# Attention over 4096 positions: energies in three float32r passes, with q and k streamed from HBM

## The chip, the cores and the metric

The kernel runs on one core of a Trainium2 chip. The metric is the device time of one execution in microseconds (us). Runs were called fast at a mean granted clock of 0.98 or more (the granted clock is the share of its full clock that TensorE gets). Names used below: TensorE (PE) multiplies matrices into PSUM, a memory of banks, VectorE (DVE) and ScalarE (ACT) work element by element, GpSimd (POOL) issues some of the DMAs. PEld is TensorE's loading of weights. A ring is a set of buffers used in turn. float32r is a form of float32 whose matmuls cost TensorE less. A "record" is one line of the trace for one executed instruction.

## The reference

```python
B, W, H, C = x.shape            # 4, 64, 64, 256
N = W * H                       # 4096
q = einsum('bwhc,cd->bwhd', x, Wq) + bq      # d = 128
k = einsum('bwhc,cd->bwhd', x, Wk) + bk
v = einsum('bwhc,cd->bwhd', x, Wv) + bv
pq, pk, pv = (t.reshape(B, -1, N) for t in (q, k, v))
energy = einsum('bcn,bcm->bnm', pq, pk)
attention = softmax(energy, axis=-1)
out = einsum('bcm,bnm->bcn', pv, attention).reshape(B, W, H, C)
return gamma * out + x
```

## The kernel before

Each of the 4 images is projected first (16 iterations of transpose, qk, v). Then 16 groups of 256 columns follow, each of 8 steps of 512 keys, so 512 steps in all. A step makes energies in full f32 (4 matmuls), exponentiates them on ScalarE, splits the result into float32r parts `h`, `l`, `d`, and multiplies these with the parts of v (24 matmuls). At a group's end the two sums are scaled, transposed and added to x. The program itself sets the order of work on every engine.

```python
ps_s = pool("ps_s", 4, space=PSUM)     # four one-bank score buffers
ps_o = pool("ps_o", 1, space=PSUM)     # four accumulators a0 b0 a1 b1
# ... (cut)
def energy(b, u):
    # ...
    for k in range(2):
        sp = ps_s.tile([P, 2, NB], F32, tag="s", ...)
        for i in range(2):
            nc.tensor.matmul(sp[:, i, :], pr.pk[:, 4 * t + 2 * k + i, :],
                             pr.pqf[:, g * NB : (g + 1) * NB], start=True, stop=True)
        nc.scalar.activation(x[:, 2 * k : 2 * k + 2, :], sp, AF.Exp)
    nc.scalar.activation(h, x, AF.Identity, scale=UPPER)
# ... (cut)
for u in range(STEPS):
    if u + LOOK < STEPS:
        energy(b, u + LOOK)
    proceed()                  # one piece of the finish of an earlier group
    if u + 1 < STEPS:
        halves(b, u + 1)       # l and d of the next step, VectorE
    attend(b, u)               # 24 matmuls; scales the sums at a group's end
    proceed()
```

## Time and profile before

| | before |
|---|---|
| time, median | 2666.6 us |
| TensorE busy | 2639 us, 99% |
| VectorE / ScalarE busy | 1507 us / 1334 us (57% / 50%) |
| one step of 8 energy records and 24 attention matmuls | 4.58 us |
| one group of 8 steps | 37.22 us |
| one iteration of the projection | 3.89 us |
| from an image's first to its last scaling of sums | 556.6 us |
| from there to the next image's first | 104.1 us |

The prediction shows how the page is read. The slices of the span add one thing, that nothing varies over the run except the DMA's work in the four projections (each digit is a fortieth of the span in tenths; PEclk is the granted clock of TensorE):

```profile
PE   8999999999999999999999999999999999999998
PEclk9999999999999999999999999999999999999999
DMA  2000000000200000000020000000002000000000
```

### The profile page before, as it was taken

Reading aid. Unit: us, or ns where it says so; the run is one execution under the profiler, and the core shown is the slowest. Engines: PE = TensorE matmul, PEld = TensorE weight load, DVE = VectorE, ACT = ScalarE, POOL = GpSimd, SP = SyncE. Lnnn points to the kernel's source line nnn. Section 1 sums busy time; section 2 is a strip of 40 time slices with the busy share of each in tenths; the row PEclk is TensorE's granted clock in tenths of the full one; section 3 lists DMA queues with packets and bytes.
Section 4 is the critical chain, followed back from the end, with each engine's and each line's share of the span. In section 5 each row is a group of like instructions: output and inputs, shape, how many; then the busy total and the mean of one; then the engine's idle time right before and its main releaser. Section 6 shows DMA issues by size and latency. Waiting matters only on the chain.

```text
span 2665.1 us, 42006 instructions
## 1 busy us (share of the span) xinstructions
PE 2639.4 (99%) x17922; PEld 2486.4 (93%) x17922; DVE 1506.8 (57%) x1993; ACT 1333.7 (50%) x1922; POOL 44.8 (2%) x70
## 2 busy tenths in 40 slices
PE   8999999999999999999999999999999999999998
PEld 7999999999899999999989999999998999999998
DVE  3555555555465555555545555555555555555555
ACT  3555555455455455455445555455545555545543
POOL 0000000000000000000000000000000000000000
PEclk9999999999999999999999999999999999999999
DMA  2000000000200000000020000000002000000000
GB/s 89 9 16 10 17 17 17 13 13 17 72 9 17 13 13 16 17 17 9 17 72 9 17 17 9 17 17 17 17 17 64 9 17 17 17 9 17 17 9 10
DMA packets 41667, 53.76 MB, mean 20 GB/s; under 512 B 3584, under 2 KB 37376, under 8 KB 41472
## 3 DMA queue, kind: packets, MB, share of 16 engines
q1 hardware_dynamic: 34816, 33.56, 4.1%
q0 software_dynamic: 5120, 16.78, 1.8%
q8 instruction: 142, 2.33, 0.3%
q10 hardware_dynamic: 1536, 0.66, 0.1%
q14 instruction: 53, 0.43, 0.0%
HBM read 34.21 MB, written 16.78 MB: 19 GB/s over the span
## 4 chain that ended last, share of the span: by engine, by line
PE 98%; DVE 1%; ACT 0%; DMA 0%; issue 0%; POOL 0%; ACTq 0%
PE a L294 37%; PE s L250 33%; PE b L294 18%; PE qk L136 4%; PE v L156 4%; PE ot L330 1%; PE xt L123 1%; DMA bv_sb<-in_L_conv_bv_dram 0%; DVE d L268 0%; DVE l L265 0%; ACT v L165 0%; ACT o L319 0%; DMA wqk_sb<-in_L_conv_Wk_dram 0%; DVE vl L238 0%; ACT vh L235 0%; DVE o L322 0%
## 5 line engine op out<-in xcount | busy, mean ns | idle before, releaser
L294 PE MATMUL a<-vh,h 128*128 128x258 f32 x4096 | 1242.3, 303 | 0.0
L294 PE MATMUL a<-vl,l 128*128 128x258 f32 x4096 | 1156.2, 282 | 1.9 <-DVE l L265 1.9
L294 PE MATMUL b<-vd,d 128*128 128x256 f32 x4096 | 1151.3, 281 | 3.0 <-DVE d L268 3.0
L257 ACT ACTIVATE x<-s 128x512 f32<-128x512 f32 x1024 | 610.5, 597 | 1056.2 <-PE s L250 1042.6
L265 DVE TENSOR_TENSOR l<-x,h 128x1024 fp32r<-128x1024 f32 x512 | 626.5, 1224 | 844.4 <-issue 841.8
L250 PE MATMUL s<-pq,pk 128*128 128x256 f32 x4096 | 966.5, 379 | 0.0
L250 PEld LDWEIGHTS s<-pq,pk 128*128 128x128 f32 x4096 | 741.2, 190 | 80.3
L294 PEld LDWEIGHTS a<-vl,l 128*128 128x128 f32 x4096 | 773.1, 189 | 14.5 <-DVE l L265 3.1
L294 PEld LDWEIGHTS a<-vh,h 128*128 128x128 f32 x4096 | 773.6, 189 | 11.5
L294 PEld LDWEIGHTS b<-vd,d 128*128 128x128 f32 x4096 | 774.0, 189 | 3.8 <-DVE d L268 3.8
L268 DVE SCALAR_TENSOR_TENSOR d<-h,x 128x1024 fp32r<-128x1024 f32 x512 | 623.9, 1219 | 0.0
L259 ACT ACTIVATE h<-x 128x1024 fp32r<-128x1024 f32 x512 | 542.7, 1060 | 16.3
L136 PE MATMUL qk<-wqk_sb,xts 128*128 128x256 f32 x512 | 123.5, 385 | 7.7 <-ACT xts L129 7.7
L156 PE MATMUL v<-xts,wv_sb 128*128 128x256 f32 x512 | 119.7, 379 | 0.0
L319 ACT ACTIVATE o<-b,r 128x256 f32<-128x256 f32 x128 | 60.6, 474 | 108.2 <-DVE r L313 108.2
L136 PEld LDWEIGHTS qk<-wqk_sb,xts 128*128 128x128 f32 x512 | 93.9, 193 | 19.4 <-ACT xts L129 8.8
L156 PEld LDWEIGHTS v<-xts,wv_sb 128*128 128x128 f32 x512 | 97.3, 190 | 13.2
L238 DVE SCALAR_TENSOR_TENSOR vl<-vh,v 128x512 fp32r<-128x512 f32 x64 | 44.4, 693 | 113.1 <-ACT vh L235 113.1
L165 ACT ACTIVATE v<-v,bv_sb 128x256 f32<-128x256 f32 x128 | 53.6, 469 | 105.6 <-PE v L156 105.6
L322 DVE SCALAR_TENSOR_TENSOR o<-a,r,o 128x256 f32<-128x256 f32 x128 | 62.0, 484 | 52.6 <-ACT o L319 52.6
L334 POOL DMA_DIRECT2D out_dram<-x x64 | 44.1, 690 | 2613.3 <-DVE x L333 2575.5
L333 DVE TENSOR_TENSOR x<-x,ot 128x512 f32<-128x512 f32 x64 | 44.0, 687 | 39.1 <-PE ot L330 39.1
(32 smaller groups left out, 406.1 us busy)
## 6 DMA issues: line engine op xcount, KB each, us to landing
x<-in_x_dram SPq DMA_DIRECT2D x128, 256.0 KB, 2.9
out_dram<-x POOLq DMA_DIRECT2D x64, 256.0 KB, 2.5
wv_sb<-in_L_conv_Wv_dram ACTq DMA_DIRECT2D x1, 256.0 KB, 4.4
wqk_sb<-in_L_conv_Wq_dram ACTq DMA_DIRECT2D x1, 128.0 KB, 2.1
wqk_sb<-in_L_conv_Wk_dram ACTq DMA_DIRECT2D x1, 128.0 KB, 3.1
bqk_sb<-in_L_conv_bq_dram ACTq DMA_DIRECT2D x1, 64.0 KB, 5.5
bqk_sb<-in_L_conv_bk_dram ACTq DMA_DIRECT2D x1, 64.0 KB, 5.8
bv_sb<-in_L_conv_bv_dram ACTq DMA_DIRECT2D x2, 0.5 KB, 5.1
```

What stands on the lines that cost most here:

```text
L136: nc.tensor.matmul(qk[:, s, :], self.xt[i][:, k, s, :], wqk_sb[:, k, :], start=(k == 0), stop=(k == KC - 1),)
L156: nc.tensor.matmul(vp[:, eh, :], wv_sb[:, k, eh * P : (eh + 1) * P], self.xt[i][:, k].rearrange("p s a -> p (s a)"), start=(k == 0), stop= ...
L165: nc.scalar.activation(to[:, eh, :], vp[:, eh, :], AF.Identity, bias=bias[:, eh : eh + 1], scale=scale,)
L238: nc.vector.scalar_tensor_tensor(t[:, m, :C], h.bitcast(F32), -f, v4, ALU.mult, ALU.add)
L250: nc.tensor.matmul(sp[:, i, :], pr.pk[:, 4 * t + 2 * k + i, :], pr.pqf[:, g * NB : (g + 1) * NB], start=True, stop=True,)
L257: nc.scalar.activation(x[:, 2 * k : 2 * k + 2, :], sp, AF.Exp)
L259: nc.scalar.activation(h, x, AF.Identity, scale=UPPER)
L265: nc.vector.tensor_tensor(l, x, h.bitcast(F32), ALU.subtract)
L268: nc.vector.scalar_tensor_tensor(d, h.bitcast(F32), 1.0 + E, x, ALU.mult, ALU.subtract)
L294: nc.tensor.matmul(out_, left[:, i, n], right[:, m, :], start=(m == 0 and first), stop=(m == NM - 1 and last),)
L319: nc.scalar.activation(o[:, j, :], bb, AF.Identity, scale=r[:, 0, j : j + 1])
L322: nc.vector.scalar_tensor_tensor(o[:, j, :], a[:, :C], r[:, 1, j : j + 1], o[:, j, :], ALU.mult, ALU.add)
```

## The change

The intent is to take the energies out of full f32. q and k are each split into an upper half and two differences ("forms"). Three float32r products then give two sums, `sa` and `sb`, and the exponential of the energy is the product of two exponentials. The three forms of k and of q aren't kept on the chip: the projection writes them to HBM and each step loads its k forms (768 KB). The score ring of four PSUM banks becomes two rings of two. The order at a group's end changes: the halves of the next step now come between the two halves of `attend`. Two settings change too: energies run three steps ahead instead of two (LOOK), and v lags the qk of the projection by one iteration instead of three (LAG), so one v instead of three is left for an image's start.

```diff
-        ps_s = pool("ps_s", 4, space=PSUM)
+        ppool, work, kpool = pool("ppool", 2), pool("work", 2), pool("kpool", 3)
+        dram = pool("dram", 2, space=DRAM)
+        ps_s = pool("ps_s", 2, space=PSUM)
 ... (cut)
+        def project_qk(b, i):
+            ...
+            nc.scalar.activation(h, x, AF.Identity, scale=UPPER / 64)
+            for j, s, op in ((1, -64.0, ALU.add), (2, 64.0 * (1.0 + E), ALU.subtract)):
+                nc.vector.scalar_tensor_tensor(f[:, :, j, :], h.bitcast(F32), s, x, ALU.mult, op)
+            nc.gpsimd.dma_start(kf[b][i // 2, :, i % 2], f[:, 1])
+            nc.gpsimd.dma_start(qf[b]..., f[:, 0])
 ... (cut)
+            for i in range(2):
+                for to, f, first, last in ((sa, 0, True, False), (sa, 1, False, True), (sb, 2, True, True)):
+                    nc.tensor.matmul(to[:, i], kt[:, 2 * k + i, f, :], q[:, :, f, :], start=first, stop=last)
+            for to, sp, scale in ((x, sa, (1.0 + E) / E), (y, sb, -1.0 / E)):
+                nc.scalar.activation(to[...], sp, AF.Exp, scale=scale)
+        def join(b, u):
+            nc.vector.tensor_tensor(x, x, y, ALU.mult)
 ... (cut: start of an image)
+            load_q(b, 0)
+            for u in range(3):
+                load_k(b, u)
 ... (cut: the loop of steps)
+                if ahead < STEPS:
+                    energy(b, ahead, 0)
+                if u + 2 < STEPS:
+                    join(b, u + 2)
+                    upper(b, u + 2)
                 proceed()
+                attend(b, u, 0)            # at a group's end: scales half j=0
                 if u + 1 < STEPS:
                     halves(b, u + 1)
-                attend(b, u)
+                if ahead < STEPS:
+                    energy(b, ahead, 1)
+                    load_k(b, ahead + 2)
                 proceed()
+                attend(b, u, 1)            # at a group's end: scales half j=1
```

## The prediction

> **What bounds the kernel now.** I read the page's busy shares first, then the chain of work that ended last, then the costliest groups, and last the timeline of one steady stretch. From the page:
>
> ```profile
> PE 2639.4 (99%) x17922; PEld 2486.4 (93%) x17922; DVE 1506.8 (57%) x1993; ACT 1333.7 (50%) x1922; POOL 44.8 (2%) x70
> ...
> PE 98%; DVE 1%; ACT 0%; DMA 0%; issue 0%; POOL 0%; ACTq 0%
> ...
> L294 PE MATMUL a<-vh,h 128*128 128x258 f32 x4096 | 1242.3, 303 | 0.0
> ...
> L257 ACT ACTIVATE x<-s 128x512 f32<-128x512 f32 x1024 | 610.5, 597 | 1056.2 <-PE s L250 1042.6
> L265 DVE TENSOR_TENSOR l<-x,h 128x1024 fp32r<-128x1024 f32 x512 | 626.5, 1224 | 844.4 <-issue 841.8
> L250 PE MATMUL s<-pq,pk 128*128 128x256 f32 x4096 | 966.5, 379 | 0.0
> ```
>
> TensorE is the bound and waits for almost nothing (idle 0.0 before its groups); 98% of the ending chain is TensorE. VectorE and ScalarE are idle nearly half the time, waiting for it. A mean of 303 or 379 ns is a pipelined duration, not a cost, so I price matmuls by start-to-start distance. The TensorE timeline of one step (512 steps in all: 4 images x 16 groups x 8):
>
> ```profile
> 1006.59 1.89 PE L250 MATMUL s<-pq,pk 128*128 128x256 f32 x8
> ...
> 1011.17 1.89 PE L250 MATMUL s<-pq,pk 128*128 128x256 f32 x8
> ```
>
> A step takes 4.58 us. Its 8 energy records are 4 program matmuls (2048 in the source, 4096 records); the chain gives such a run 1.73 us, so one f32 matmul costs 0.433 us. The other 2.85 us are 24 float32r matmuls: 0.119 us each. Eight steps and one output transpose (about 0.6 us) make 37.22 us, the distance between the like points 1001.45 and 1038.67; no wait shows in it. An image takes 663.5 us (first qk matmuls at 674.18 and 1337.68): 16 groups are 595.5, the projection 16 x 3.89 = 62.2, start and drain some 5.
>
> VectorE at the end of a group, where the sums are scaled:
>
> ```profile
> 1037.32 0.16 DVE L311 COPY zall<-a 128x1 f32<-128x1 f32 x1 [0.74 <-PE a L294]
> ...
> 1038.48 0.48 DVE L322 SCALAR_TENSOR_TENSOR o<-a,r,o 128x256 f32<-128x256 f32 x1 [0.41 <-ACT o L319]
> 1038.88 0.15 DVE L311 COPY zall<-a 128x1 f32<-128x1 f32 x1
> ...
> 1041.14 0.69 DVE L333 TENSOR_TENSOR x<-x,ot 128x512 f32<-128x512 f32 x1 [0.64 <-PE ot L330]
> 1041.75 1.22 DVE L265 TENSOR_TENSOR l<-x,h 128x1024 fp32r<-128x1024 f32 x1
> 1042.88 1.22 DVE L268 SCALAR_TENSOR_TENSOR d<-h,x 128x1024 fp32r<-128x1024 f32 x1
> ```
>
> One scaling holds VectorE in order for 1.56 us (1037.32 to 1038.88), 0.4 of it waiting for ScalarE. A 1024-wide operation costs 1.135 us back to back (1041.75 to 1042.88). Today TensorE doesn't feel this, because halves for the next step are ready long before.
>
> **What the Trainium skill says.** "FP8 and Floating Point Precision", TensorE Precision Notes: true FP32 takes four passes through the array. Here 0.433 against 0.119 us is a ratio of 3.65; the trace agrees roughly, as each float32r matmul costs some 0.01 us more than its share. "PSUM — Partial Sum Buffer", Specifications: eight banks of 512 FP32 values. The kernel before has four one-bank score buffers and four accumulators, so two kinds of score force the rings down to two each. "VectorE: DVE Perf Modes", The TRN2 errata: an fp32 tensor-tensor takes (N+151)/0.96 ns, 1224 ns at N = 1024; the trace shows 1224 ns, so I use it for the new product. "DMA: Bandwidth & Descriptors", Anatomy of one DMA: some 2.0 us plus bytes/436 GB/s on the GpSimd path, 2.6 us for 256 KB; the trace's stores landed in 2.5 us.
>
> **The change, part by part.**
>
> 1. Energies. 4 f32 matmuls (1.73 us) become 12 float32r ones (12 x 0.119 = 1.42). TensorE's step is 4.27 us, 0.305 less; x 512 = **-156 us**. This is the whole intended gain.
>
> 2. ScalarE per step: 4 exponentials instead of 2. 4 x 0.597 + 1.06 = 3.45 us of 4.27. Hidden, 0.8 to spare. VectorE per step: product, l and d, 3 x 1.135 = 3.41 us. Hidden in mid-group. Over a group VectorE has 27.2 + 2 x 1.56 + 0.61 = 31.0 us of some 34.8: no bound on average, but close.
>
> 3. End of a group. Program order on VectorE is now: product for u+2, scaling of half j=0 (after TensorE ends that half), **then** the halves for u+1, then scaling of j=1. I worked one group with the durations above, time 0 being the start of the last step's energies. TensorE ends half j=0 at 0.71 + 1.42 = 2.14. VectorE, done with the product at 1.3, waits; it scales from 2.29 to 3.85, makes l to 5.07 and d to 6.2. TensorE wants d at 4.27 + 0.71 + 0.24 = 5.2 and gets it at 6.3: 1.1 us lost. Then VectorE scales j=1 from 6.12 to 7.68; ScalarE's o for it stands in the queue in front of the next exponentials, which come at 7.25 instead of about 5. Product of u+3 to 8.9, its h to 10.1, second pair of exponentials to 11.1. Meanwhile the transpose has taken a slot of the two-deep "b" ring, so the next energies need just that second pair: 0.2 to 0.5 us lost there and as much at the transpose. Step u+3 starts at 15.2; 3 x 4.27 + 0.6 = 13.4 would be free of waits. Some 1.8 us per group; for the 60 group ends inside an image **+108 us**.
>
> 4. Projection. Transposes, qk and v share a ring of two banks. The next qk needs the bank that v used: two ScalarE copies, released about 0.2 + 0.84 + 0.05 = 1.09 us after v ends, while the transpose between covers 0.43. 0.66 us x 15 x 4 = **+40 us**. The new h and two differences per iteration (ScalarE 0.6, VectorE 1.2 us more) fit in 4.5 us.
>
> 5. Start of an image. Before, energies followed the last qk at once. Now: bias add 0.9 us, h 0.7, two differences 1.3, four GpSimd issues (0.7 each in the trace), then two writes and two loads, 2.0 MB, at the 350 GB/s that the stores show (16.78 MB in 1.8% of the span) 5.6 us, and landing: about 10.5 us after the last qk, of which v covers 1.7. Then exponentials, product, h and halves of the first units run nearly in series, some 11 us with 6 us of matmuls in them. About 8.7 + 5 us idle, less what start and drain cost today: +12 us, x 4 = **+48 us**. A cold clock after the gap could add a little.
>
> 6. Streaming. One k load is 786 KB a step, q 393 KB a group: 0.4 GB, 190 GB/s of the 350 seen. A buffer comes free and is asked for more than two steps ahead (some 10 us), against an estimated 2 + 1.8 + queueing: hidden.
>
> Sum: 2666.6 - 156 + 108 + 40 + 48 = **2707 us**.
>
> **Rivals.**
> - A: TensorE stays fed, only the projection and the start cost something: 2666.6 - 156 + 60 = about 2570. For it: 99% busy before, and averages of 80 to 90% on the other engines leave room. Against it: at the group's end the room is 1.2 us and the delay over 2.
> - B: VectorE becomes the bound through most of a group, as its 31 us plus waits grow past TensorE's: 2750 to 2800. For it: two waits for TensorE and ScalarE per group stand in its order. Against it: mid-group it regains 0.86 us a step, so it recovers in three steps.
> - C: the loads don't keep up (casting to float32r on the way, or slow issue). If a load took over 4.3 us in the stream, every step would wait, and the time would leave the range upward. The trace shows stores of that path at 350 GB/s, no loads.
>
> **Range and chances.** The -156 us is the firmest term. The 108 may be 60 to 140 (the 1.1 us wait for d follows from order alone), the 40 from 20 to 55, the 48 from 25 to 80. These put most of the weight from 2615 to 2770. I widen downward, since a schedule so deliberately split may have been tuned to avoid what I see. Range 2585 to 2775. Faster by over 2% means under 2613: 0.23. Slower means over 2720: 0.35.
>
> **What will tell.** Energy groups of 12 matmuls 1.42 us long confirm part 1. Part 3 shows as TensorE waiting for d or l about 1 us just after each group's end, with smaller waits for PSUM a step later, and the eight-step period near 36.6 instead of 37.22; a period of 34.8 refutes it. Part 4 shows as an iteration of about 4.5 us instead of 3.89. Part 5 shows as a TensorE gap of 8 to 12 us between an image's last v matmuls and its first energies, with DMA as releaser. TensorE waiting for k loads in mid-group would make the whole sum wrong.

## The result, and the profile after

The changed kernel takes 2742.5 us (median of 4, 2741.7 to 2744.8) against 2666.4 us (median of 4) in the same rounds: ratio 1.0288, 95% interval 1.0270 to 1.0305, slower. (Ratios here are the mean time of one kernel's fast runs over the mean of the other's in the same rounds, so not quite the ratio of the medians.) The result is correct.

The page of the changed kernel, its busy shares, chain, slices, and the groups that answer to those shown of before:

```profile
PE 2539.8 (93%) x19970; PEld 2461.6 (90%) x19970; DVE 2159.8 (79%) x2568; ACT 1809.9 (66%) x3010; POOL 443.0 (16%) x774
...
PE   7799999999979999999987999999998799999998
...
PEclk9899999999999999999998999999999899999999
DMA  6666556665666665566476666665647566666653
...
PE 65%; DVE 13%; ACT 13%; DMA 5%; issue 3%; POOL 1%; ACTq 0%; SPq 0%; DVEq 0%; POOLq 0%
...
L308 DVE TENSOR_TENSOR x<-x,y 128x1024 f32<-128x1024 f32 x512 | 626.2, 1223 | 265.6 <-ACT y L298 265.6
...
k<-kf POOLq DMA_DIRECT2D x512, 768.0 KB, 4.7
```

TensorE is busy 100 us less than before, yet the run is 76 us longer: the chain that ended last is now only 65% TensorE, with 13% each of VectorE and ScalarE, and 5% DMA. No engine is a bound on average. The time is lost in waits, and the slices say where to look first: TensorE's 7s and 8s stand at the four image starts, and its clock is a little lower at three of them.

In the stream, the intended gain is there. A step in mid-group takes 4.26 us (two energies' starts 883.22 and 887.48), where 4.27 was predicted and 4.58 was before. A typical group takes 36.4 us instead of 37.22 (the median distance of like points; below, 824.20 to 860.59), so most of what the steps gain is lost again inside the group. VectorE's timeline around the end of one group, in order of start (start, duration, then what ended the idle time before it):

```profile
824.20 0.16 DVE L365 COPY zall<-a 128x1 f32<-128x1 f32 x1 [1.20 <-PE a L347]
...
858.16 1.23 DVE L308 TENSOR_TENSOR x<-x,y 128x1024 f32<-128x1024 f32 x1 [0.78 <-ACT y L298]
860.59 0.16 DVE L365 COPY zall<-a 128x1 f32<-128x1 f32 x1 [1.20 <-PE a L347]
...
861.74 0.48 DVE L370 SCALAR_TENSOR_TENSOR o<-a,r,o 128x256 f32<-128x256 f32 x1 [0.41 <-ACT o L369]
862.14 1.21 DVE L319 TENSOR_TENSOR l<-x,h 128x1024 fp32r<-128x1024 f32 x1
863.28 1.22 DVE L322 SCALAR_TENSOR_TENSOR d<-h,x 128x1024 fp32r<-128x1024 f32 x1
864.41 0.15 DVE L365 COPY zall<-a 128x1 f32<-128x1 f32 x1
```

And TensorE's timeline at the same place:

```profile
864.64 0.36 PE L347 MATMUL b<-vd,d 128*128 128x256 f32 x1 [0.84 <-DVE zall L365]
...
869.35 0.39 PE L294 MATMUL sb<-q,k 128*128 128x256 f32 x1 [0.48 <-ACT y L298]
```

VectorE sits idle for 1.20 us until TensorE has ended half j=0, then scales it, and only then makes `l` and `d`. `d` ends at 864.50 (863.28 + 1.22), and TensorE's first matmul with it starts 0.14 us later. The reader names the small copy `zall`, which came last by its count, but the matmul reads `d`. A step later the energies wait for a bank of the `sb` ring until ScalarE has exponentiated it. In start times these two cost TensorE about 1.1 and 0.6 us per group (the idle time in the bracket is less, since the end of a matmul is modelled).

The other part lies between the streams. From the reciprocals' start times, summed over the run:

| part | before, us | after, us | difference |
|---|---|---|---|
| start of the run to image 0's first scaling | 116.1 | 144.2 | +28.1 |
| first to last scaling, four images | 2226.4 | 2189.4 | -37.0 |
| last scaling to the next image's first, three times | 312.4 | 395.2 | +82.8 |
| last scaling to the end | 10.1 | 12.7 | +2.6 |
| span of the profiled runs | 2665.1 | 2741.5 | +76.4 |

In these parts the projection's iteration is 4.65 us instead of 3.89, with this wait each time (TensorE's timeline, two lines of before and two of after):

```profile
43.82 1.89 PE L136 MATMUL qk<-wqk_sb,xts 128*128 128x256 f32 x8
...
47.71 1.89 PE L136 MATMUL qk<-wqk_sb,xts 128*128 128x256 f32 x8
```

```profile
57.68 1.99 PE L135 MATMUL qk<-wqk_sb,xts 128*128 128x256 f32 x8 [0.49 <-ACT v L165]
...
62.33 1.99 PE L135 MATMUL qk<-wqk_sb,xts 128*128 128x256 f32 x8 [0.49 <-ACT v L165]
```

The qk matmul waits until ScalarE has copied v out of the bank that it wants. The view of waits has this 52 times in the run, 13 an image (`PEld qk L135 <- ACT v L165: 36.7, 52, 0.8`). Then comes the image's start, again TensorE's timeline of the first image:

```profile
81.57 1.89 PE L156 MATMUL v<-xts,wv_sb 128*128 128x256 f32 x8
94.81 0.76 PE L294 MATMUL sa<-q,k 128*128 128x256 f32 x2 [11.35 <-DMA k<-kf]
...
105.15 0.80 PE L294 MATMUL sa<-q,k 128*128 128x256 f32 x2 [3.73 <-ACT x L298]
...
109.44 0.80 PE L294 MATMUL sa<-q,k 128*128 128x256 f32 x2 [1.30 <-ACT x L298]
```

After the v matmuls TensorE stands for 11.35 us until the first k forms have gone out to HBM and come back, then waits twice more for exponentials. The busy time by stretch (columns: window, its length, busy time and count of PE, PEld, DVE, ACT, POOL, then the granted clock, the DMA share and GB/s):

```profile
83.30:94.80 11.50, 0.16 (x1) 0.02 (x1) 2.76 (x5) 1.99 (x4) 3.61 (x6) 0.68 0.92 284
94.80:109.40 14.60, 9.38 (x44) 8.48 (x44) 5.24 (x6) 8.19 (x15) 2.02 (x4) 0.73 0.50 170
109.40:116.20 6.80, 6.75 (x36) 6.76 (x37) 4.43 (x5) 4.68 (x8) 0.62 (x2) 0.60 0.54 173
116.20:120.50 4.30, 4.30 (x39) 4.30 (x39) 3.49 (x4) 3.12 (x5) 0.53 (x1) 1.00 0.51 183
```

Three stretches pass at a granted clock of 0.60 to 0.73. The first step takes 6.8 us; the next has the full clock and takes 4.3. The other images start alike, but their first step is less slow: from its first attention matmul to that of the second step it is 6.0 us in the first image, and 4.3, 5.1 and 5.2 in the others. Two lines of VectorE's timeline are needed later:

```profile
101.70 0.69 DVE L263 SCALAR_TENSOR_TENSOR vd<-vh,v 128x512 fp32r<-128x512 f32 x1
102.31 1.22 DVE L308 TENSOR_TENSOR x<-x,y 128x1024 f32<-128x1024 f32 x1
```

### The profile page after: what moved, and what is told of

It reads as the page before. It is cut to its first block, busy times and chain, and to the rows that moved or that the text cites. A ratio compares the mean times of both kernels' runs of the same rounds, so it can differ in the third digit from the quotient of the medians.

```text
span 2741.5 us, 50093 instructions
## 1 busy us (share of the span) xinstructions
PE 2539.8 (93%) x19970; PEld 2461.6 (90%) x19970; DVE 2159.8 (79%) x2568; ACT 1809.9 (66%) x3010; POOL 443.0 (16%) x774
## 4 chain that ended last, share of the span: by engine, by line
PE 65%; DVE 13%; ACT 13%; DMA 5%; issue 3%; POOL 1%; ACTq 0%; SPq 0%; DVEq 0%; POOLq 0%
PE a L347 25%; PE sa L294 13%; PE b L347 12%; PE sb L294 7%; DMA k<-kf 4%; PE qk L135 4%; ACT h L313 4%; PE v L156 4%; DVE l L319 3%; DVE d L322 3%; DVE x L308 3%; ACT y L298 2%; ACT o L369 2%; ACT v L165 2%; ACT x L298 1%
## 5 line engine op out<-in xcount | busy, mean ns | idle before, releaser
L347 PE MATMUL b<-vd,d 128*128 128x256 f32 x4096 | 1158.1, 283 | 50.7 <-DVE zall L365 50.5
L347 PE MATMUL a<-vh,h 128*128 128x258 f32 x4096 | 1163.1, 284 | 0.0
L298 ACT ACTIVATE x<-sa 128x512 f32<-128x512 f32 x1024 | 609.2, 595 | 522.0 <-PE sa L294 491.3
L294 PE MATMUL sa<-q,k 128*128 128x256 f32 x4096 | 776.3, 282 | 74.1 <-DMA k<-kf 52.5
L308 DVE TENSOR_TENSOR x<-x,y 128x1024 f32<-128x1024 f32 x512 | 626.2, 1223 | 265.6 <-ACT y L298 265.6
L294 PEld LDWEIGHTS sa<-q,k 128*128 128x128 f32 x4096 | 636.2, 191 | 81.0 <-issue 56.4
L294 PE MATMUL sb<-q,k 128*128 128x256 f32 x2048 | 583.0, 285 | 28.4 <-ACT y L298 28.4
L298 ACT ACTIVATE y<-sb 128x512 f32<-128x512 f32 x1024 | 608.2, 594 | 0.0
L278 POOL DMA_DIRECT2D k<-kf x512 | 278.5, 544 | 1483.3 <-PE sb L294 1468.3
L294 PEld LDWEIGHTS sb<-q,k 128*128 128x128 f32 x2048 | 389.8, 190 | 41.0 <-ACT y L298 41.0
L135 PE MATMUL qk<-wqk_sb,xts 128*128 128x256 f32 x512 | 129.0, 395 | 31.7 <-ACT v L165 24.2
L135 PEld LDWEIGHTS qk<-wqk_sb,xts 128*128 128x128 f32 x512 | 93.4, 192 | 56.7 <-ACT v L165 36.7
```

The lines of the kernel that those rows point to most:

```text
L135: nc.tensor.matmul(qk[:, s, :], self.xt[i][:, k, s, :], wqk_sb[:, k, :], start=(k == 0), stop=(k == KC - 1),)
L278: nc.gpsimd.dma_start(t.rearrange("p (i s) f d -> p i s (f d)", s=2), kf[b][u % NU])
L294: nc.tensor.matmul(to[:, i], kt[:, 2 * k + i, f, :], q[:, :, f, :], start=first, stop=last)
L298: nc.scalar.activation(to[:, 2 * k : 2 * k + 2, :], sp.rearrange("p i j d -> p i (j d)"), AF.Exp, scale=scale,)
L308: nc.vector.tensor_tensor(x, x, y, ALU.mult)
L347: nc.tensor.matmul(out_, left[:, i, n], right[:, m, :], start=(t == 0 and start_), stop=(t == NU - 1 and stop),)
```

## The experiments

Nine kernels, each an edit of the changed kernel. My theory: the loss is in the order of VectorE's work at a group's end, in the shared PSUM ring in the projection, and in the chain of forms, writes and loads at an image's start. The rivals: too much VectorE work, the stream from HBM, and the lowered clock. The changed kernel was not run again in the rounds of these experiments; the kernel before was, with 2666.3 us in the rounds of e1, e3, e4 and e6 and 2665.7 us in the others, so differences to 2742.5 us hold to a few us.

### e1_order: halves before the scaling

```diff
-                attend(b, u, 0)
                 if u + 1 < STEPS:
                     halves(b, u + 1)
+                attend(b, u, 0)
```

> The only edit: VectorE makes l and d of the next step before it scales half j=0, instead of after. Theory (the order on VectorE is the cause of the group-end loss): TensorE no longer waits about 1.1 us for d at a group's end; the scaled sums come later, so the new group's first matmuls may wait some 0.3 us for them, and 0.4 us at the sb ring stay. Group period from 36.4 to about 35.4 us, total about 2685 us (2665 to 2700). Rival (the amount of VectorE work, not its order): the wait only moves to another matmul, the group period stays above 36.1 and the total within 15 us of 2742.

Measured: 2662.8 us median (2662.1 to 2668.4), ratio to the kernel before 0.9994 (0.9977 to 1.0010): the same. Moving two lines takes 80 us away; the group period is 35.1 us. The gain was larger than expected, and the median falls just below the expected range: I had reckoned 0.3 us of waiting for the scaled sums, but no such wait shows, and the wait at the sb ring is down to 0.3 us. The rival is refuted: the work is the same, only its order differs. The table's streams shrink by 80.2 us, so all of it is there.

### e3_noproduct: less VectorE work in the old order

```diff
-            nc.vector.tensor_tensor(x, x, y, ALU.mult)
```

> Wrong result on purpose: the product of the two exponentials is left out, so VectorE has a third less work (3 x 1.14 to 2 x 1.14 us a step) in the same order. Theory (order): the wait of about 1.1 us for d just after a group's end stays in full, because VectorE still may not start l before TensorE has ended half j=0 and the scaling is through; only the later wait at the sb ring (0.6 us) goes. Group period about 35.8 us, total about 2705 us. Rival (VectorE overloaded): with a third of its work gone all group-end waits vanish, group period about 34.7, total about 2640 us.

Measured: 2672.9 us (2 runs, 2671.7 and 2674.1), ratio 1.0025 (1.0005 to 1.0045). What the second sum contributes is within the tolerance. The view of waits of this run:

```profile
PE b L346 <- DVE zall L364: 50.6, 60, 0.8
```

TensorE's wait for `d` is what it is in the changed kernel, where the same view gives 50.5 us in 60 times, although VectorE does a third less. The group period is 35.7 us, as the theory said (35.8). So this wait is the order's; the later one, at the sb ring, is gone. The total fell by 70 us and not by 37. The reciprocals place 49 us inside the streams (42 of it by the shorter period) and some 20 outside: the part between two images is 126.5 to 127.0 us against 130.2 to 132.7, so the product stands in the chain at an image's start too, which I had left out. The amount of VectorE's work isn't free, then: it makes the wait at the sb ring and a part of the start, but not the wait for `d`.

### e6_noload: no stream of k

```diff
-            if u < STEPS:
+            if 3 <= u < STEPS:
+                loads[b, "k", u] = loads[b, "k", u % 3]
+            elif u < STEPS:
```

> Wrong result on purpose: only the first three k tiles of an image are loaded and then reused, so the stream of 768 KB a step is gone and everything else stays. Theory (the stream is hidden, except for some late loads): the group period stays at 36.4 us, only the 14 late loads of about 0.6 us go, total 2730 to 2738 us. Rival (streaming from HBM costs the time): group period under 35.8, total under 2700 us.

Measured: 2729.4 us (2 runs), wrong result as intended. Removing 0.4 GB of loads gives 13 us. The waits for `d` and at the sb ring stay (50.6 and 28.1 us in all). First to last scaling takes 544.3 us an image instead of 547.4 on average, so loads that came late cost 3 us an image, 12 in all. The rival that streaming costs the time is refuted: at most these 13 us are its.

### e4_ring: a second ring for qk

```diff
-            qk = pool.tile([P, 2, 2 * C2], F32, tag=tag, ...)
+            qk = pool.tile([P, 2, 2 * C2], F32, tag=self.qtag, ...)   # "b" where xt and v use "a"
```

> The only edit: in the projection qk takes its PSUM bank from the second ring (b), so transposes and v have the first ring (a) to themselves. Theory (the shared ring of two makes qk wait for the copies of v): an iteration falls from 4.65 to about 3.9 us, 15 x 4 x 0.76 = 46 us, total about 2697 us. Rival (ScalarE, VectorE or the writes of the forms set the iteration): it stays above 4.3 us and the total above 2720.

Measured: 2705.6 us (2703.2 to 2707.6), ratio 1.0144 (1.0127 to 1.0161), 37 us less. The iteration is 3.89 us, as before the change:

```profile
47.56 1.89 PE L136 MATMUL qk<-wqk_sb,xts 128*128 128x256 f32 x8
...
51.46 1.89 PE L136 MATMUL qk<-wqk_sb,xts 128*128 128x256 f32 x8
```

The ring was the cause of the whole 0.76 us. The 46 us of the expectation counted 15 waits an image; there are 13, which makes 39.5 us. From first to last qk the four projections are 40 us shorter, and 37 arrive: the gap before the first energies grows from 11.35 to 11.76 us in the first image, and to 12.3 at its longest (2.9 us more in all four).

### e5_early: loads before the last forms

```diff
-            f = kpool.tile([P, 4, 3, P], F32R, tag="k", ...)
+            f = kpool.tile([P, 4, 3, P], F32R, tag="f", ..., bufs=2)
 ... (in the projection's loop)
+                if i in (8, 9, 10):
+                    load_k(b, i - 8)
+                if i == 11:
+                    load_q(b, 0)
-            load_q(b, 0)
-            for u in range(3):
-                load_k(b, u)
```

(o, v4 and qks, which have one shape, share a ring of three to make room.)

> The fresh forms get two buffers of their own (o, v4 and qk share one ring of three to make room), so that the first k and q loads of an image go out in the middle of the projection instead of after its last form. Theory (the gap at an image's start is the chain forms, writes, loads): the gap of 11.4 us between the last v matmuls and the first energies goes, the clock is not lowered after it, some 15 to 18 us an image in all, total about 2675 us (2665 to 2690). Rival (the start is bound by exponentials, product and halves in series, the gap only hides it): under 6 us an image, total above 2715.

Measured: 2702.7 us (2696.9 to 2706.3), ratio 1.0143 (1.0126 to 1.0160): 40 us less, 10 an image instead of 15 to 18. The expected range was missed, and so was the rival's. The gap of 11.4 us is gone: in the first image the energies start at 84.38, right behind v. But the waits for exponentials that follow are unchanged (3.73 us once more), and in the stretch from 94.80 to 109.40 the granted clock is 0.77. The gap hid next to nothing of this series, and the clock is low behind the series without the gap too.

### e9_warm: the array kept busy in the gap

```diff
+            w = ps_s.tile([P, 2, NB], F32, tag="b", name=f"w_{b}")
+            for _ in range(88):
+                nc.tensor.matmul(w[:, 0, :], vh[:, 0, :P], vh[:, 0, :NB], start=True, stop=True)
```

> 88 dummy float32r matmuls are put into the gap before an image's first energies; nothing else changes. Theory (part of what the start costs is the lowered clock after 11 us of idling: a step of 6.8 us instead of 4.26 and slower energies before it): the granted clock stays near 1.0 through the start, some 4 to 6 us an image, total 2718 to 2728 us. Rival (the clock is not on the path there, the series of ScalarE and VectorE is): total within 5 us of 2742.

Measured: 2739.7 us (2737.2 to 2740.6), ratio 1.0276 (1.0259 to 1.0293): 3 us less, within what the rival said. In the first image the gap passes at a clock of 1.00, but the next stretch is at 0.73 again:

```profile
83.30:94.80 11.50, 11.50 (x97) 11.47 (x96) 2.92 (x5) 2.01 (x5) 3.61 (x6) 1.00 0.93 295
94.80:109.40 14.60, 9.34 (x48) 8.37 (x47) 6.53 (x7) 10.04 (x19) 2.11 (x4) 0.73 0.59 200
```

The parts outside the streams shrank by 7 us in all, and more late loads in the streams took back 3. So what the gap does to the clock is worth some 2 us an image at most, a size that the spread of the runs doesn't make firm; behind the waits in series the granted clock is low a second time. The test isn't quite clean: in three images the energies start 14.00 us after the last qk with no wait in front, so there the dummies themselves set that time (13.19 to 14.97 us in the changed kernel).

### e10_split: VectorE's order at a group's end, with l and d before and between the scaling

```diff
                 if u + 1 < STEPS:
-                    halves(b, u + 1)
+                    lower(b, u + 1)               # l
+                attend(b, u, 0)
+                if end:
+                    half = ratio(b, u // NU, 0)   # the four small operations
+                    scale_b(*half)                # ScalarE's part
+                if u + 1 < STEPS:
+                    diff(b, u + 1)                # d
+                if end:
+                    scale_a(*half)                # VectorE's sum
```

(Half j=1 likewise around the next product; the transpose comes later.)

> VectorE's work at a group's end is put in another order only: l, then the four small operations of half j=0, d, then the sum of that half; half j=1 likewise around the next product; the transpose is two half-steps later. Theory: no wait of TensorE is left at a group's end, group period 34.8 us (8 x 4.27 + 0.6) against 36.4 and 35.1 with the halves merely first, total about 2645 us (2638 to 2655). Rival (VectorE or PSUM still hold the end of a group): period 35.1 or more, total 2660 or more.

Measured: 2622.7 us (2620.6 to 2623.6), ratio 0.9839 (0.9823 to 0.9856), 120 us less than the changed kernel. The group period is 34.6 us, and in the stretch from 200 to 640 us the view of TensorE's waits is empty. The longest waits of TensorE that name a releaser, over the whole run, are now these:

```profile
PE sa L294 <- DMA k<-kf: 42.5, 4, 10.9
PEld qk L135 <- ACT v L165: 36.7, 52, 0.8
PE qk L135 <- ACT v L165: 24.2, 49, 0.6
```

All are of the projection and the image's start. All 120 us are in the streams by the reciprocals. That is 22 us more than expected: the late loads went too, worth 12 us by e6_noload (only the 4 waits for k at the starts remain), and the period is 0.2 us under my sum, another 12 in 60 periods. Why the loads are no longer late was not tried by itself.

### e11_all and e12_start: everything together

The first puts e10_split, e4_ring and e5_early together and lets the halves of unit 0 come before the product of unit 1.

> Split order, the second ring for qk, early loads, and halves of unit 0 before the product of unit 1 at the start, all together. Theory: the four costs are separate and add up: 2742 - 96 (groups) - 40 (ring) - 68 (start) - some 10 (order at the start) = about 2528 us (2510 to 2550), 5% under the kernel before. Rival (one hides another): above 2570 us.

Measured: 2557.8 us (2557.1 to 2559.3), ratio 0.9595 (0.9579 to 0.9611). It beats both kernels, by 4% and by 185 us, but misses the expected range: the three single gains (120, 37 and 40 us) would make 2546. ScalarE's timeline shows where some of it went. The form of an iteration waits for the write of the form two before, which stands behind the early loads (17 such waits, 49.6 us in all; TensorE's share shows in the projections, which take 251 us from first to last qk in all four, where e4_ring took 230: 21 us, more than the 12 that are missing):

```profile
61.87 0.63 ACT L245 ACTIVATE f<-qks 128x512 fp32r<-128x512 f32 x1 [4.05 <-DMA qf<-f]
```

The next edit spreads the loads and moves the last v behind the first units' work:

```diff
-                if i in (8, 9, 10):
-                    load_k(b, i - 8)
-                if i == 11:
+                if i in (5, 8, 11):
+                    load_k(b, (i - 5) // 3)
+                if i == 13:
                     load_q(b, 0)
 ... (start of an image)
+            for u in range(LOOK):
+                for k in range(2):
+                    energy(b, u, k)
+                if u:
+                    upper(b, u - 1)
+                    load_k(b, u + 2)
+                if u < 2:
+                    join(b, u)
+            halves(b, 0)
+            for i in range(NI - LAG, NI):
+                project_v(b, i)
```

> As the kernel with all four edits, but the early loads are spread over every third iteration of the projection, and at an image's start the energies of units 0 to 2 run ahead, the products and halves of unit 0 follow at once, and the last v comes after them. Theory: in the kernel with all edits the halves of a form waited for the write of the form two before (two waits of 4 us an image, as the loads stood in front of the writes), and the first attention matmuls waited for work of the last v; without both some 10 us an image go, total about 2517 us (2505 to 2530). Rival (the waits only move, the start stays serial): 2545 us or more.

Measured: 2545.4 us (2544.8 to 2547.0), ratio 0.9550 (0.9534 to 0.9566), 4.5% under the kernel before. 12 us went, not 40: the expected range was missed, and the median stands at the edge of what the rival said. The start itself is shorter, from the first energies to the first attention matmul 9.8 to 11.4 us an image instead of 15.6 to 17.5, as it would be if the last v stood in the way there (the edit moves the products and halves too, so v alone isn't shown). But the first energies now wait 0.9 to 2.1 us for q, and the view of waits shows the wait for writes, which only moved:

```profile
ACT f L245 <- DMA qf<-f: 57.2, 22, 4.4
PEld v L157 <- ACT v L166: 24.7, 37, 3.1
PE v L157 <- ACT v L166: 13.8, 11, 2.7
```

Two buffers for fresh forms are still too few beside the loads, wherever these stand. A third was not tried.

## Why the prediction was right, point by point

The measured 2742.5 us lies inside the range of 2585 to 2775, and the direction of the point (2707, above before) was right, though it stood in "within 2%" and the result is 2.9% slower. The distance of 35 us has one main source, the start of an image; other errors are small or cancel.

1. **Energies, -156.** Right. The step is 4.26 us where 4.27 was worked out.
2. **ScalarE and VectorE hidden in mid-group.** Right: VectorE waits 0.78 us a step for exponentials, where 0.86 was predicted to spare, and the product takes 1223 ns where 1224 was taken.
3. **End of a group, +108 (1.8 us each).** Right in cause and nearly in size: 36.4 - (8 x 4.26 + 0.6) = 1.7 us. The wait for `d` costs the 1.1 us that were worked out. The second wait is at the sb ring, 0.6 us, and none at the transpose, where 0.2 to 0.5 at each was said. e1_order and e10_split show that the order is the cause, as the work stays the same; e3_noproduct shows that a third less work leaves the wait for `d`, though not the wait at the ring, as it was. The streams as a whole were predicted at -38 us (120 steps of four images at -0.305, +108) and came out at -37.0 partly by luck: the period is 36.4 us and not 36.6, 11 us in all, and late loads take 12.
4. **Projection, +40.** Right in cause, and in size by two errors that cancel: each wait costs 0.76 us and not 0.66 (4.65 us an iteration against the predicted 4.5), but there are 52 of them and not 60, so 39.5 us in all. e4_ring gives 37 of it back.
5. **Start of an image, +48.** This is the term that was too small. In the first image the first energies came 13.2 us after the last qk (94.81 - 81.57), not 10.5; step 0 came 14.6 us after them (109.44 - 94.81), not "some 11 us"; and it took 6.8 us, not 4.3. The excess is 2.7 + 3.6 + 2.5 = 8.8 us in this image. The others differ in the parts (their first step is less slow), so the sum comes from the table: outside the streams the run grew by 113.5 us; with the 9.8 us that the four first groups gain (32 steps of 0.305), and without the projection's 40, the starts and the drain cost 83 us where 48 was said, 35 too much. The step of the prediction that was mis-sized is the gap and the series behind it, the series most. The timeline shows the first product starting at 102.31, 7.5 us after the first energies: in VectorE's order the two halves of the last v stand in front of it (the second starts at 101.70), and they wait for v matmuls that come later. The cold clock, which "could add a little", covers this stretch and step 0 at 0.60 to 0.73; the 2.5 us of step 0 are all the clock's, since TensorE is busy 6.75 of 6.80 us there. e5_early removes the gap and leaves this series, e12_start, which takes the last v out of it and moves the products and halves too, shortens it; e9_warm shows that keeping the array busy in the gap alone doesn't help, as the clock is low again behind the series.
6. **Streaming hidden.** Right in the main, by e6_noload; late loads cost 12 us, where none was predicted. The GpSimd queue moved 495 MB in 56.0% of the span, 322 GB/s while busy, where 350 was taken.

Of the rivals, A (TensorE stays fed) fell at the group's end. B (VectorE the bound through most of a group) fell with e1_order, where the same work in another order gives 80 us back, and with VectorE's waits of 0.78 us in mid-group, although the result came within 8 us of its 2750 to 2800. C (loads don't keep up) fell with e6_noload. Two small readings were off without effect: the line shown puts VectorE's idle time to issue and not to TensorE, and the upper ends of the three terms make 2786 us and not 2770. What stays open: why the late loads vanish in e10_split, and what the clock costs at a start by itself, since no run held it at 1.00 through the series.

## What to carry to other kernels

When one engine's program order holds both the work that feeds the bound and work that waits for the bound, put the feeding work first and the waiting work into its gaps: here much the same instructions in another order were worth 120 us, most of the 156 us that the change was to gain. Averages of 80% on the other engines say nothing of this; work one turn of the loop by hand with the durations of the trace, and do the same for the start of each phase. A round trip through memory between two phases should be started before the last item of the first phase, with buffers enough that its writes don't hold the phase up.

## What the Trainium skill lacked or had wrong

- "FP8 and Floating Point Precision" has four passes for true FP32, but no page gives a time for a float32r matmul. Here one of 256 columns costs 0.118 us back to back, against 0.108 us for each pass of an f32 matmul (0.433 / 4), so three float32r passes are 0.82 of an f32 matmul (0.355 / 0.433).
- "DMA: Bandwidth & Descriptors", Anatomy of one DMA, fits one DMA with 2.0 us plus bytes/436 GB/s; an estimate from it is 3.8 us for the 768 KB of k. What the section doesn't give is the spread in a busy stream: here, with 56.0% of the DMA engines' time on that queue, the median was 4.7 us and the longest 9.5 us.
